# A decoder layer with gated delta-rule attention on one Trainium2 core: block-wise substitution on fewer rows, one sum of squares instead of two, and part of the work moved between engines

## The chip, the cores and the metric

The kernel runs on one core of a Trainium2 chip. A core has TensorE (matmuls; the profile calls it PE, its weight loads PEld), VectorE (DVE), ScalarE (ACT), GpSimd (POOL) and SyncE (SP), which here only issues DMAs. Each engine works through its own queue in order; engines wait for each other by semaphores. The metric is the device time of one execution in microseconds.

## The reference

Input `x` is 16 sequences of 128 tokens with 256 features. The layer is: gated delta-rule attention with 16 key heads and 32 value heads of width 128, then cross attention, then a mixture of experts, each followed by a sum with its input and a layer norm. The change touches the attention alone. Cut to what matters:

```python
mixed = hidden_states @ w_qkv                 # then a causal convolution of 4 taps, silu
q, k, v = jnp.split(mixed, [KEY_DIM, 2 * KEY_DIM], axis=-1)
q = _l2norm(q) * DK ** (-0.5)                 # each key head serves two value heads
k = _l2norm(k)
def step(Sm, inp):
    q_, k_, v_, g_, b_ = inp                  # g_: log of the decay, b_: beta
    Sm = Sm * jnp.exp(g_)[..., None, None]
    kv = jnp.einsum('bhk,bhkv->bhv', k_, Sm)
    delta = (v_ - kv) * b_[..., None]
    Sm = Sm + jnp.einsum('bhk,bhv->bhkv', k_, delta)
    o = jnp.einsum('bhk,bhkv->bhv', q_, Sm)
    return (Sm, o)
og = o * jax.nn.silu(z)
on = og * jax.lax.rsqrt(jnp.mean(og * og, axis=-1, keepdims=True) + EPS) * norm_w
return on.reshape(B, S, VAL_DIM) @ w_out
```

## The kernel before

**Units and steps.** The 128 steps of the recurrence are written as a triangular system of 128 tokens per sequence and head. The work is cut into 64 units: a unit is one key head (with its two value heads, r = 0 and 1) for four sequences (`G` = 4, index b). Four units form a group (`U` = 4). The main loop (from L549) runs over s and works in each step on units of several ages: `a` = unit s (keys, queries, decay, products), `v` (values, six units later), `m`, `p`, `q` (the solution in blocks, seven to nine units later) and `o` (output, ten units later). The order within a step on TensorE, VectorE, ScalarE and SP is chosen by a scheduler when the program is built; GpSimd's order is the order of the code (`manual_schedule`, L548).

**Blocks.** The 128 tokens are four blocks of 32. `products` (L395) makes `lp`, the products of keys with keys and with queries times the decay, and copies the four diagonal 32x32 blocks of the key products to `ldg`. `clear` (L414) then writes zeros over the diagonal blocks 1 to 3 in `lp`, on GpSimd, one step later. What stands above the diagonal is zero by the decay.

**Substitution and solution.** Twice a step, `substitute` (L494) takes off what the blocks before contribute, and `solve` (L510) multiplies with the inverse of the diagonal block. `substitute` has three jobs (unit, r, block st), with st = 1, 2 and 3. For each b and job one matmul (L504) goes to the 32 rows of `pu` that belong to the block. Its operands have all 128 rows: rows of later blocks meet zeros in `lp`. VectorE subtracts `pu` from `u` (L508). `solve` does 16 matmuls (L519) of 32 rows and 32 columns, and ScalarE copies the results back (L523). The profile writes the shape that a matmul takes of the array as rows*columns: L504 is 128*32, L519 is 32*32.

**Inverse.** The inverses of a group's 128 diagonal blocks are made together, one per partition. `begin` (L226) prepares `bp` (beta over the squared norm of the key) and `T` (transposed `ldg`) on VectorE; GpSimd then multiplies `T` by `nbp` (L251), does 30 steps j (`step`, L262: a product and a sum each) and `end` (L271: ones on the diagonal, times `bp`). `turn` (L277) transposes the result on VectorE. The 30 steps are cut into pieces over three steps of the main loop (`piece`, L559). `bp` has one buffer.

**Norms.** `norms` (L370) squares the queries on ScalarE, sums them over the 128 features by four matmuls with ones (`pss`, L377), and VectorE transposes and scales the sums to `ss`. `rms` (L462) sums the squares of the output in the same way (`pms`, L467), with 1/128 as weights, transposes, and adds `ss`; `rms_end` (L476) raises to the power -1/2 on GpSimd, to `rstd`, which VectorE needs for the output (L490). In GpSimd's queue `rms_end` stands behind `piece(0)` and `clear`.

**Output weights.** `scale_wo` (L162) runs in steps 2 to 9: two loads of `w_out`, a multiplication by the norm's weight on GpSimd (L170), two stores to device memory. Its tile shares the one buffer of `og2`.

Of the kernel before, what the change touches and what calls it, by code (L numbers as in the profile page):

```python
# [8 lines left out]
F32 = mybir.dt.float32  # L9
# [32 lines left out]
def decoder_kernel(  # L42
# [16 lines left out]
    ones = const.tile([P, BS], F32, name="ones")  # L59
    pool.memset(ones, 1.0)  # L60
# [56 lines left out]
    with ExitStack() as st:  # L117
# [100 lines left out]
        class Group:  # L218
# [7 lines left out]
            def begin(self):  # L226

                k = self.k

                def small(tag, **kw):  # L230
                    return sb.tile([P, BS], F32, tag=tag, name=f"{tag}{k}", **kw)

                g, h0 = k * U // HK, k * U % HK * 2
                bg = small("bg", bufs=1)
                vec.tensor_copy(bg.rearrange("p (h b) -> p h b", b=G),
                                beta[:, g * G : (g + 1) * G, h0 : h0 + 2 * U]
                                .rearrange("p b h -> p h b"))
                self.bp = bp = small("bp", bufs=1)
                vec.transpose(bp, bg)
# [12 lines left out]
                sst = small("sst", bufs=1)  # L252
                vec.transpose(sst, ss)
                self.sst = sst

# [6 lines left out]
            def step(self, j):  # L262
                T = self.T
                n = BS - 1 - j
                tmp = sb.tile([P, 256], F32, tag="tmp", bufs=1, name=f"tmp{self.k}_{j}")
                tv = tmp[:, : n * j].rearrange("p (i c) -> p i c", c=j)
                pool.tensor_tensor(tv, bc(T[:, j + 1 :, j : j + 1], [P, n, j]),  # L267
                                   bc(T[:, j : j + 1, 0:j], [P, n, j]), ALU.mult)
                pool.tensor_tensor(T[:, j + 1 :, 0:j], T[:, j + 1 :, 0:j], tv, ALU.add)  # L269
# [15 lines left out]
        class Unit:  # L285
# [84 lines left out]
            def norms(self):  # L370

                sq = self.t([P], "sq", bufs=1)
                act.activation(sq, self.kq[:, :, 1, :], AF.Square)
                pss = sm_pool.tile([P, G, BS], F32, tag="sm", name=f"pss{self.n}")
                for i in range(NB):
                    blk = slice(i * BS, (i + 1) * BS)
                    pe.matmul(pss[blk].rearrange("p b t -> p (b t)"), lhsT=ones, rhs=sq[:, :, blk],  # L377
                              start=True, stop=True)
                sst = self.t([BS], "sqt", bufs=1)
                vec.transpose(sst, pss)  # L380
                self.ss = self.t([], "ss", bufs=DELAY + 5)
                vec.tensor_scalar(self.ss, sst[:, :, 0], 1e-6, 1e-6 * P, ALU.add, ALU.mult)
# [30 lines left out]

            def clear(self):  # L414
                for i in range(1, NB):
                    blk = slice(i * BS, (i + 1) * BS)
                    pool.memset(self.lp[blk, :, :, 0, blk].rearrange("p r b t -> p (r b) t"), 0.0)
# [32 lines left out]
            def attend(self, r):  # L450

                if r == 0:
                    self.og = self.t2("og")
                    self.og2 = self.t2("og2", bufs=1)
# [5 lines left out]
                act.activation(self.og2[:, r], self.og[:, r], AF.Square)  # L460

            def rms(self):  # L462

                pms = sm_pool.tile([P, 2, G, BS], F32, tag="sm", name=f"pms{self.n}")
                for i in range(NB):
                    blk = slice(i * BS, (i + 1) * BS)
                    pe.matmul(pms[blk].rearrange("p r b t -> p (r b t)"), lhsT=inv_dv,  # L467
                              rhs=self.og2[:, :, :, blk].rearrange("p r b t -> p (r b) t"),
                              start=True, stop=True)
                mst = sb.tile([P, 2, G, BS], F32, tag="mst", bufs=1, name=f"mst{self.n}")  # L470
                vec.transpose(mst.rearrange("p r b t -> p (r b t)"),
                              pms.rearrange("p r b t -> p (r b t)"))
                self.var = var = sb.tile([P, 2, G], F32, tag="var", name=f"var{self.n}")
                vec.tensor_tensor(var, mst[:, :, :, 0], bc(self.ss[:, None, :], [P, 2, G]), ALU.add)  # L474
# [18 lines left out]

        def substitute(name, jobs):  # L494
# [6 lines left out]
            for b in range(G):  # L501
                for u, r, st in jobs:
                    blk = slice(st * BS, (st + 1) * BS)
                    pe.matmul(pu[blk, b, :], lhsT=u.lp[:, r, b, 0, blk], rhs=u.u_[r][:, b, :],  # L504
                              start=True, stop=True)
# [38 lines left out]
        PIECES = 5  # L544
        done = None


        with tc.manual_schedule(engines={mybir.EngineType.Pool}):  # L548
            for s in range(NU + DELAY + 3):  # L549
# [9 lines left out]
                def piece(i):  # L559
# [3 lines left out]
                    total = 3 * PIECES - 2  # L563
                    if at_ == 0:
                        inv.begin()
                    for j in range(1 + 30 * at_ // total, 1 + min(30, 30 * (at_ + 1) // total)):
                        inv.step(j)
                    if at_ == 2 * PIECES - 1:
                        inv.norms()
                    if at_ == total - 1:  # L570
# [39 lines left out]
                if q is not None:  # L610
                    q.attend(0)
# [14 lines left out]
                if q is not None:  # L626
                    q.attend(1)
                if p is not None:
                    p.gate(1)
                if a is not None:  # L630
                    a.norms()
# [648 lines left out]
```

## Time and profile before

| what | value |
|---|---|
| median of 9 runs | 2244.73 us (2236.57 to 2247.95) |
| profiled execution, own time | 2242.45 us |
| its span, first to last instruction | 2240.4 us |
| granted TensorE clock, mean | 0.969 |
| TensorE's idle time in 300 to 1500 us | 48.4 of 1200 us |
| `pu` (L504) on TensorE, 300 to 1500 us | 2184 passes, 101.4 us |
| `clear` (L417) on GpSimd, 300 to 1500 us | 138 memsets, 42.0 us |
| VectorE's idle time ended by GpSimd's `end` (L275), 300 to 1500 us | 33.0 us, 9 times |
| VectorE's idle time ended by `rstd` (L478), 300 to 1500 us | 43.7 us, 12 times |

The attention takes the first 1797 us; its steady stage begins near 200 us. Cross attention and the experts follow. Times in the traces are microseconds from the span's start. A row of the order in time merges equal instructions that follow each other: start, duration from the first start to the last end, engine, line, operation, written and read tiles, array shape, operand shape, count; in brackets the idle time before and what ended it. Two fp32 passes make one matmul, and each is counted. Matmul ends are modelled and can overlap the next start, so prices below are taken from start to start.

### The profile page before, as it was taken

The page shows a single profiled execution, that of the slowest core. Times are in us where ns is not written, and L with a number is a line of the kernel's source. Part 1 is how long each engine was busy: PE and PEld are TensorE (multiplying, and loading weights), DVE is VectorE, ACT ScalarE, POOL GpSimd, SP SyncE. Part 2 cuts the span into 40 slices and gives each one's busy share as a digit, 9 for nine tenths or more (in the row PEclk, how much of TensorE's full clock was granted, in tenths as well). Part 3 has the DMA queues.
Part 4 walks back from the last instruction along what each step waited for, and adds up shares of the span by engine and source line. Part 5 has one row for each costly group of instructions (what it writes and reads, how often), then busy time and mean ns, then how long its engine had stood idle before and what let it go on. Part 6 is the DMA issues. An engine that isn't in the chain of part 4 may idle for free. (4 is left out here: it accounts for less than half of the span.)

```text
span 2240.4 us, 41392 instructions
## 1 busy us (share of the span) xinstructions
PE 2065.3 (92%) x15128; PEld 1254.5 (56%) x15128; DVE 1747.0 (78%) x3247; ACT 1330.7 (59%) x2692; POOL 1123.8 (50%) x1679
## 2 busy tenths in 40 slices
PE   5659999999999999999999999999999969999997
PEld 3335555555555556555555556555655634448874
DVE  5757888888898888888888888898856667766545
ACT  4646666666666666666666666666655435554431
POOL 1658373646556473829373646556482143252222
PEclk9889999999999999999999999999999979999998
DMA  6332221122222212222221222222111070013321
GB/s 168 109 103 59 66 62 58 58 62 66 57 67 62 57 57 65 64 57 63 61 62 57 57 58 69 60 62 62 34 29 38 20 259 1 1 50 100 105 86 57
DMA packets 140664, 150.78 MB, mean 67 GB/s; under 512 B 14184, under 2 KB 111472, under 8 KB 140464
## 3 DMA queue, kind: packets, MB, share of 16 engines
q1 hardware_dynamic: 135760, 139.56, 21.6%
q0 software_dynamic: 3072, 8.39, 1.2%
q8 instruction: 122, 2.00, 0.4%
q14 instruction: 78, 0.64, 0.1%
q10 hardware_dynamic: 1632, 0.19, 0.1%
HBM read 125.82 MB, written 22.28 MB: 66 GB/s over the span
## 5 line engine op out<-in xcount | busy, mean ns | idle before, releaser
L523 ACT COPY u<-pt 32x512 f32<-32x512 f32 x512 | 294.5, 575 | 63.7 <-PE pt L519 53.7
L359 POOL TENSOR_TENSOR yv<-yv,y2v 128x508 f32<-128x508 f32 x128 | 161.8, 1264 | 272.7 <-DVE yv L351 266.9
L508 DVE TENSOR_TENSOR u<-u,pu 32x512 f32<-32x512 f32 x384 | 263.5, 686 | 33.3 <-PE pu L504 21.5
L490 DVE SCALAR_TENSOR_TENSOR acc<-pp,rstd,acc 128x256 f32<-128x256 f32 x512 | 222.2, 477 | 83.0 <-POOL rstd L478 77.2
L269 POOL TENSOR_TENSOR Tp<-Tp,tmp 128x30 f32<-128x30 f32 (+14 forms) x480 | 266.0, 554 | 37.6
L486 PE MATMUL pp<-wo,og 128*128 128x256 f32 x1024 | 273.8, 394 | 0.0
L334 PE MATMUL pjkq<-xT,wkq 128*128 128x512 f32 x512 | 247.6, 625 | 24.6 <-issue 20.0
L351 DVE SCALAR_TENSOR_TENSOR ykq<-pjkq,cw,ykq 128x500 f32<-128x500 f32 (+2 forms) x384 | 262.7, 726 | 6.1 <-ACT ykq L344 4.3
L334 PE MATMUL pjz<-xT,wz 128*128 128x512 f32 x512 | 251.5, 615 | 12.5 <-DVE yv L351 12.0
L334 PE MATMUL pjv<-xT,wv 128*128 128x512 f32 x512 | 249.7, 610 | 12.1 <-DVE ykq L351 6.6
L267 POOL TENSOR_TENSOR tmp<-Tp 128x30 f32<-128x30 f32 (+14 forms) x480 | 245.9, 512 | 28.2
L351 DVE SCALAR_TENSOR_TENSOR yv<-pjv,cw,yv 128x504 f32<-128x504 f32 (+1 forms) x256 | 188.0, 734 | 66.7 <-ACT y2v L348 62.5
L486 PEld LDWEIGHTS pp<-wo,og 128*128 128x128 f32 x1024 | 182.9, 190 | 84.4 <-issue 62.0
L519 PE MATMUL pt<-u,Tt 32*32 32x128 f32 x4096 | 176.5, 274 | 17.9 <-DVE u L508 17.7
L519 PEld LDWEIGHTS pt<-u,Tt 32*32 32x32 f32 x4096 | 117.1, 105 | 125.1 <-ACT ykq L344 38.7
L360 ACT ACTIVATE vT<-yv 128x512 f32<-128x512 f32 x128 | 80.2, 627 | 168.3 <-POOL yv L359 168.3
L334 PEld LDWEIGHTS pjkq<-xT,wkq 128*128 128x128 f32 x512 | 94.6, 196 | 143.1 <-issue 130.0
L406 DVE TENSOR_TENSOR lp<-pk,e 128x512 f32<-128x512 f32 x256 | 159.4, 681 | 13.9 <-PE pk L403 13.8
L478 POOL TENSOR_TENSOR rstd<-var,m_half 128x8 f32<-128x8 f32 x64 | 105.4, 1648 | 126.0 <-DVE var L474 122.7
L446 ACT ACTIVATE u<-pv,nk 128x128 f32<-128x128 f32 x512 | 149.3, 369 | 32.5 <-PE pv L443 30.6
L389 DVE TENSOR_TENSOR_SCAN e<-dec,ident 128x512 f32<-128x512 f32 x128 | 163.2, 1316 | 2.4 <-DMA dec<-dec_d 0.6
L457 PE MATMUL po<-lp,u 128*128 128x128 f32 x1024 | 147.7, 285 | 17.1 <-DVE acc L490 17.1
(227 smaller groups left out, 3683.0 us busy)
## 6 DMA issues: line engine op xcount, KB each, us to landing
dec<-dec_d SPq DMA_DIRECT2D x64, 512.0 KB, 5.1
wkq<-in_L_attn_w_qkv_dram SPq DMA_DIRECT2D x128, 128.0 KB, 3.5
wv<-in_L_attn_w_qkv_dram SPq DMA_DIRECT2D x64, 256.0 KB, 2.8
wz<-in_L_attn_w_z_dram SPq DMA_DIRECT2D x64, 256.0 KB, 2.7
wo<-wo_d SPq DMA_DIRECT2D x64, 256.0 KB, 2.7
rx<-xg SPq DMA_DIRECT2D x44, 128.0 KB, 2.1
yg<-ry SPq DMA_DIRECT2D x44, 128.0 KB, 1.7
xg<-zero SPq DMA_DIRECT2D x10, 512.0 KB, 8.0
```

What stands on the lines that cost most here:

```text
L267: pool.tensor_tensor(tv, bc(T[:, j + 1 :, j : j + 1], [P, n, j]), bc(T[:, j : j + 1, 0:j], [P, n, j]), ALU.mult)
L269: pool.tensor_tensor(T[:, j + 1 :, 0:j], T[:, j + 1 :, 0:j], tv, ALU.add)
L334: pe.matmul(pj.rearrange("p b t -> p (b t)"), lhsT=ws[kc], rhs=xTs[self.g][:, kc, :], start=(kc == 0), stop=(kc == 1))
L351: vec.scalar_tensor_tensor(out=y[:, :, d:], in0=pj[:, :, : P - d], scalar=c[:, k : k + 1], in1=y[:, :, d:], op0=ALU.mult, op1=ALU.add)
L359: pool.tensor_tensor(y[:, :, 1:], y[:, :, 1:], y2[:, :, 1:], ALU.add)
L389: vec.tensor_tensor_scan(out=e.rearrange("p b t -> p (b t)"), data0=self.dec[:, r, :], data1=ident4.rearrange("p b t -> p (b t)"), initial ...
L406: self.made = vec.tensor_tensor(self.lp[:, r, hf * 2 : hf * 2 + 2], pk, bc(self.e[r][:, hf * 2 : hf * 2 + 2, None, :], [P, 2, 2, P]), ALU. ...
L486: pe.matmul(pp[:, r, :], lhsT=self.og[:, r, b, :], rhs=self.wo[:, r, :], start=True, stop=True)
L490: vec.scalar_tensor_tensor(out=a, in0=pp[:, r, :], scalar=self.rstd[:, r, b : b + 1], in1=a, op0=ALU.mult, op1=ALU.add)
L508: vec.tensor_tensor(u.u_[r][blk], u.u_[r][blk], pu[blk], ALU.subtract)
L519: pe.matmul(pt[blk, b, :], lhsT=groups[u.n // U].Tt[blk, 8 * u.u + G * r + b, :], rhs=u.u_[r][blk, b, :], start=True, stop=True)
L523: act.copy(u.u_[r][blk], pt[blk])
```

## The change

- `bp` has two buffers.
- `clear` is gone. `substitute` reads only the rows ahead of the block: 32, 64 or 96 of 128.
- `norms` and `rms` become `square` and `sums`: the squares of the output of one unit and of the queries of another lie in one tile (`sqs`), and one set of four matmuls over up to 384 columns and one transpose serve both. It runs in the step after, between `decay` and `key_query(0)`. The matmuls take 1/128 as weights for both, and `ss` is scaled to match; the tile `ones` is gone.
- `rms_end` stands ahead of `piece(0)` in GpSimd's queue.
- The negation (`T` times `nbp`) is a method of its own. For group 0 it and steps 1 to 15 run on VectorE, in piece 0, and steps 16 to 30 on GpSimd in pieces 1 to 8. For the other groups the negation stands in piece 1, and the 30 steps in pieces 1 to 12.
- `scale_wo` multiplies on ScalarE, with the two buffers of `og`.

```diff
-    ones = const.tile([P, BS], F32, name="ones")
-    pool.memset(ones, 1.0)
...
-            wor = sb.tile([P, 2, G, P], F32, tag="og2", bufs=1, name=f"wor{i}")
+            wor = sb.tile([P, 2, G, P], F32, tag="og", name=f"wor{i}")
...
-            pool.tensor_scalar(wor, wor, normw, None, ALU.mult)
+            act.activation(wor, wor, AF.Copy, scale=normw)
...
-                self.bp = bp = small("bp", bufs=1)
+                self.bp = bp = small("bp")
...
-                pool.tensor_tensor(self.T, self.T, bc(nbp[:, None, :], [P, BS, BS]), ALU.mult)
+                self.nbp = nbp
...
+            def negate(self, eng):
+                eng.tensor_tensor(self.T, self.T, bc(self.nbp[:, None, :], [P, BS, BS]), ALU.mult)
...
-            def step(self, j):
+            def step(self, j, eng):
...
-            def norms(self):
-                sq = self.t([P], "sq", bufs=1)
-                act.activation(sq, self.kq[:, :, 1, :], AF.Square)
...
+            def square(self, sqs):
+                act.activation(sqs, self.kq[:, :, 1, :], AF.Square)
...
-            def clear(self):
-                for i in range(1, NB):
-                    blk = slice(i * BS, (i + 1) * BS)
-                    pool.memset(self.lp[blk, :, :, 0, blk].rearrange("p r b t -> p (r b) t"), 0.0)
...
+        def sums(name, sqs, o, a):
+            lo, hi = (0 if o is not None else 2), (3 if a is not None else 2)
+            psq = sm_pool.tile([P, 3, G, BS], F32, tag="sm", name=f"psq{name}")
+            for i in range(NB):
+                blk = slice(i * BS, (i + 1) * BS)
+                pe.matmul(psq[blk, lo:hi].rearrange("p r b t -> p (r b t)"), lhsT=inv_dv,
+                          rhs=sqs[:, lo:hi, :, blk].rearrange("p r b t -> p (r b) t"),
+                          start=True, stop=True)
+            mst = sb.tile([P, 3, G, BS], F32, tag="mst", bufs=1, name=f"mst{name}")
+            vec.transpose(mst[:, lo:hi].rearrange("p r b t -> p (r b t)"),
+                          psq[:, lo:hi].rearrange("p r b t -> p (r b t)"))
+            if o is not None:
+                o.var = sb.tile([P, 2, G], F32, tag="var", name=f"var{name}")
+                vec.tensor_tensor(o.var, mst[:, 0:2, :, 0], bc(o.ss[:, None, :], [P, 2, G]), ALU.add)
+            if a is not None:
+                a.ss = sb.tile([P, G], F32, tag="ss", bufs=DELAY + 5, name=f"ss{name}")
+                vec.tensor_scalar(a.ss, mst[:, 2, :, 0], 1e-6 / P, 1e-6 * P * P, ALU.add, ALU.mult)
...
-                    pe.matmul(pu[blk, b, :], lhsT=u.lp[:, r, b, 0, blk], rhs=u.u_[r][:, b, :],
-                              start=True, stop=True)
+                    pe.matmul(pu[blk, b, :], lhsT=u.lp[: st * BS, r, b, 0, blk],
+                              rhs=u.u_[r][: st * BS, b, :], start=True, stop=True)
...
+                    n0, last = (15, 8) if k == 0 else (0, 3 * PIECES - 3)
                     if at_ == 0:
                         inv.begin()
+                        if k == 0:
+                            inv.negate(vec)
+                            for j in range(1, 1 + n0):
+                                inv.step(j, vec)
+                        return
+                    if at_ == 1 and k > 0:
+                        inv.negate(pool)
+                    if at_ > last:
+                        return
+                    for j in range(1 + n0 + (30 - n0) * (at_ - 1) // last,
+                                   1 + n0 + (30 - n0) * at_ // last):
+                        inv.step(j, pool)
...
-                if o is not None:
-                    o.rms()
+                if o is not None or at(s - 1) is not None:
+                    sums(s, sqs, o, at(s - 1))
...
-                piece(0)
-                if s > 0 and at(s - 1) is not None:
-                    at(s - 1).clear()
                 if o is not None:
                     o.rms_end()
+                piece(0)
```

More of the change, by code (lines that the diff above doesn't have):

```diff
@@ L266, in step @@
                 tv = tmp[:, : n * j].rearrange("p (i c) -> p i c", c=j)
-                pool.tensor_tensor(tv, bc(T[:, j + 1 :, j : j + 1], [P, n, j]),
+                eng.tensor_tensor(tv, bc(T[:, j + 1 :, j : j + 1], [P, n, j]),
                                    bc(T[:, j : j + 1, 0:j], [P, n, j]), ALU.mult)
-                pool.tensor_tensor(T[:, j + 1 :, 0:j], T[:, j + 1 :, 0:j], tv, ALU.add)
+                eng.tensor_tensor(T[:, j + 1 :, 0:j], T[:, j + 1 :, 0:j], tv, ALU.add)
             def end(self):
@@ L368, in key_query @@
                 self.conv(f"kq{i}", ws, chunk, out)
-            def norms(self):
-                sq = self.t([P], "sq", bufs=1)
-                act.activation(sq, self.kq[:, :, 1, :], AF.Square)
-                pss = sm_pool.tile([P, G, BS], F32, tag="sm", name=f"pss{self.n}")
-                for i in range(NB):
-                    blk = slice(i * BS, (i + 1) * BS)
-                    pe.matmul(pss[blk].rearrange("p b t -> p (b t)"), lhsT=ones, rhs=sq[:, :, blk],
-                              start=True, stop=True)
[L379 to L382, printed above, removed]
+            def square(self, sqs):
+                act.activation(sqs, self.kq[:, :, 1, :], AF.Square)
             def decay(self):
@@ L412, in products @@
                     act.copy(grp.ldg[blk, 8 * self.u : 8 * self.u + 8, :], d)
-            def clear(self):
-                for i in range(1, NB):
-                    blk = slice(i * BS, (i + 1) * BS)
-                    pool.memset(self.lp[blk, :, :, 0, blk].rearrange("p r b t -> p (r b) t"), 0.0)
             def value(self, r):
@@ L447, in values, with attend @@
                 self.u_[r] = v
-            def attend(self, r):
+            def attend(self, r, sqs):
                 if r == 0:
                     self.og = self.t2("og")
-                    self.og2 = self.t2("og2", bufs=1)
                 po = self.bank(f"po{r}")
@@ L459, in attend @@
                 vec.tensor_tensor(self.og[:, r], po, self.zs[r], ALU.mult)
[L460 to L474, printed above, removed]
+                act.activation(sqs, self.og[:, r], AF.Square)
             def rms_end(self):
@@ L503, in substitute @@
                     blk = slice(st * BS, (st + 1) * BS)
-                    pe.matmul(pu[blk, b, :], lhsT=u.lp[:, r, b, 0, blk], rhs=u.u_[r][:, b, :],
-                              start=True, stop=True)
+                    pe.matmul(pu[blk, b, :], lhsT=u.lp[: st * BS, r, b, 0, blk],
+                              rhs=u.u_[r][: st * BS, b, :], start=True, stop=True)
             for u, r, st in jobs:
@@ L544, in decoder_kernel @@
         PIECES = 5
+        sqs = None
         done = None
@@ L562, in piece @@
                     at_ = ph * PIECES + i
-                    total = 3 * PIECES - 2
+                    n0, last = (15, 8) if k == 0 else (0, 3 * PIECES - 3)
                     if at_ == 0:
                         inv.begin()
-                    for j in range(1 + 30 * at_ // total, 1 + min(30, 30 * (at_ + 1) // total)):
-                        inv.step(j)
-                    if at_ == 2 * PIECES - 1:
+                        if k == 0:
[10 more added lines that the diff above has]
+                        inv.step(j, pool)
+                    if at_ == min(last, 2 * PIECES - 1):
                         inv.norms()
-                    if at_ == total - 1:
+                    if at_ == last:
                         inv.end()
@@ L594, in decoder_kernel @@
                     a.decay()
-                if o is not None:
-                    o.rms()
+                if o is not None or at(s - 1) is not None:
+                    sums(s, sqs, o, at(s - 1))
+                if a is not None or q is not None:
+                    sqs = sb.tile([P, 3, G, P], F32, tag="og2", bufs=1, name=f"sqs{s}")
                 if a is not None:
                     a.key_query(0)
-                piece(0)
-                if s > 0 and at(s - 1) is not None:
-                    at(s - 1).clear()
                 if o is not None:
                     o.rms_end()
+                piece(0)
                 if a is not None:
@@ L610, in decoder_kernel @@
                 if q is not None:
-                    q.attend(0)
+                    q.attend(0, sqs[:, 0])
                 if v is not None:
@@ L626, in decoder_kernel @@
                 if q is not None:
-                    q.attend(1)
+                    q.attend(1, sqs[:, 1])
                 if p is not None:
@@ L630, in decoder_kernel @@
                 if a is not None:
-                    a.norms()
+                    a.square(sqs[:, 2])
                     a.products(ga)
```

## The prediction, made before the changed kernel ran

> **What bounds the kernel now.** I read the page first (engines, then the 40 slices), then busy time by stage, then what TensorE waited for in the steady stage, and last the order in time on TensorE's matmul and weight rows.
>
> ```profile
> PE 2065.3 (92%) x15128; PEld 1254.5 (56%) x15128; DVE 1747.0 (78%) x3247; ACT 1330.7 (59%) x2692; POOL 1123.8 (50%) x1679
> ...
> PE   5659999999999999999999999999999969999997
> ```
>
> TensorE is full from the fourth slice on; only the first three slices (some 170 us) have room. By stage (columns: PE, PEld, DVE, ACT, POOL, granted clock, DMA share, GB/s):
>
> ```profile
> 134.00:200.00 66.00, 56.98 (x376) 30.47 (x376) 50.46 (x73) 41.59 (x89) 40.42 (x56) 0.95 0.32 92
> 240.00:1740.00 1500.00, 1436.03 (x11475) 872.43 (x11469) 1271.71 (x2181) 984.68 (x1984) 839.89 (x1233) 0.99 0.21 58
> 300.00:1500.00 1200.00, 1151.60 (x9172) 699.44 (x9171) 1042.31 (x1782) 795.83 (x1603) 683.21 (x1011) 0.99 0.22 61
> ```
>
> In 240 to 1740 us TensorE is busy 1436 of 1500 us, VectorE 1272, GpSimd 840. A step (one unit of 64) lasts 26 us and TensorE idles 1.1 us of it. So what relieves VectorE, ScalarE or GpSimd can gain no more than those 64 us there, and every microsecond put on TensorE is paid in full. What TensorE waited for in 300 to 1500 (engine, line, releaser: us in total, times, longest):
>
> ```profile
> PE po L457 <- DVE acc L490: 14.4, 11, 1.4
> PE pt L519 <- DVE u L508: 12.8, 24, 1.1
> PE pv L443 <- ACT vT L360: 10.2, 7, 1.5
> PE pjz L334 <- DVE yv L351: 10.1, 11, 0.9
> ```
>
> Now the price of small matmuls. Each is two passes (x24 for twelve matmuls).
>
> ```profile
> 713.75 1.07 PE L504 MATMUL pu<-u,lp 128*32 128x128 f32 x24
> 714.75 0.70 PE L486 MATMUL pp<-wo,og 128*128 128x256 f32 x2
> ...
> 188.67 0.41 PE L504 MATMUL pu<-u,lp 128*32 128x128 f32 x2
> 189.01 0.40 PE L519 MATMUL pt<-u,Tt 32*32 32x128 f32 x2
> 189.34 1.32 PE L504 MATMUL pu<-u,lp 128*32 128x128 f32 x22
> ```
>
> Start to start, twelve `pu` matmuls of one shape take 714.75 - 713.75 = 1.00 us, 0.083 each: three column strips of the array run at once. But one `pu` (shape 128*32) followed by one `pt` (32*32) takes 0.34 us, and back again 0.33, though the two use different strips. The weight row shows why:
>
> ```profile
> 188.67 0.14 PEld L504 LDWEIGHTS pu<-u,lp 128*32 128x32 f32 x2
> 189.00 0.13 PEld L519 LDWEIGHTS pt<-u,Tt 32*32 32x32 f32 x2 [0.20 <-issue]
> 189.34 1.06 PEld L504 LDWEIGHTS pu<-u,lp 128*32 128x32 f32 x22 [0.20 <-issue]
> ```
>
> At a change of shape the next weights aren't loaded until the running matmul is through (0.20 us of empty weight row, ended by no other engine). At 161.80, 162.10, 162.44 the same pattern has 0.30 and 0.34.
>
> **No clearing of blocks** (`clear`, `substitute`). `substitute` reads 32, 64 or 96 rows instead of 128. As built, its three jobs then have the shapes 32*32, 64*32 and 128*32, and the loop is over the four batches outside and the jobs inside: the shape changes at every one of the twelve matmuls of a call. Taken at the measured 0.335 us for an isolated one, a call costs 12 x 0.335 = 4.02 us instead of 1.00. There are 1536 such matmuls (64 units x 24): 1536 x (0.335 - 0.083) = **+387 us**. The trace shows 128*32 to 32*32 and back; it shows neither 32*32 to 64*32 nor 64*32 to 128*32. Upper bound 0.34 each: +394. Lower bound: nothing, as between strips of one shape (0.083). I take the upper side: all other changes of shape that I looked at (128*128 to 128*32, 128*32 to 32*32, 32*32 to 128*128) have the same 0.17 to 0.20 us gap in the weight row, and these two are of that kind. The page "TensorEngine Tiling (Array Packing)" of the Trainium skill, section "Key Properties", speaks against this edit: changing the tiling mode, and not just the tile, drains the TensorE; it lists 32x32, 64x32 and 128x32 as different modes. By its rule all twelve drain (+387 us as above); by the same-shape row alone the edit would cost TensorE nothing. The drains cover nothing and nothing covers them in the steady stage; only in the first five calls (134 to 200 us, 48 matmuls, TensorE idle 9 of 66 us) I hide half: 48 x 0.252 / 2 = **-6**. GpSimd saves three memsets of 0.30 us a unit, off TensorE's path: 0.
>
> **What frees TensorE's waits.** Two buffers for `bp`: VectorE no longer waits for GpSimd's last multiplication of the group before (33.0 us in nine waits in 300 to 1500). The power of the output norm ahead of the inverse's piece and of its wait for the negation: VectorE's `acc` no longer waits for `rstd` (43.7 us there). On TensorE these can show only in the rows above, `po` and `pjz` (24.5 of 48.3 us in 46 steps). Besides, every step gets 6 us longer for the other engines while their work stays, so part of the waits for `u` and `vT` goes too. I take 60% of the 64 us: **-38** (bounds 0 and -64). ScalarE's and VectorE's queues have that room: DVE 1272 in what would be some 1850 us.
>
> **Squares summed together.** `pss` (8 passes, 0.35 us: 725.73 to 726.08) and `pms` (8 passes: six took 0.56) become one call with 384 columns. Four strips run at once, so a call is two passes of a strip and 0.13 us around them: `pss` 2 x 0.107 + 0.13 = 0.34 and `pms` 2 x 0.213 + 0.13 = 0.56 fit; 384 columns give 2 x 0.32 + 0.13 = 0.77, that is 0.14 less than the two. x 64 = **-9** (bounds 0 and 64 x 0.35 = -22). VectorE's two transposes (450 and 314 ns) become one, about 590: hidden. The sum moves ahead of `key_query` of the next step; its consumer `ss` is used ten steps later.
>
> **Start: first inverse half on VectorE, weights scaled on ScalarE, `bp`.** (a) VectorE stood still for `bp` here:
>
> ```profile
> 132.29 0.21 DVE L239 STREAM_TRANSPOSE bp<-bg 128x32 f32<-128x32 f32 x1 [21.70 <-POOL Tp L275]
> ```
>
> But group 0 is needed anyway before unit 0 can be solved. What VectorE did between GpSimd's end (132.25) and the transpose `Tt` (138.41) can now come before: -6 at most. (b) Steps 1 to 15 and the negation leave GpSimd, where the whole took 77.96 to 132.25. On VectorE they are 30 instructions of 30 to 240 elements, at 0.18 (128x32) to 0.40 us (between 0.29 at 128 and 0.68 at 512 elements) 9.6 us, and 1.25 for the negation. They stand in VectorE's queue between the products and scans of units 4 to 6, the last behind the scan of unit 6, which puts the handing over at about 111. GpSimd's rest is 104.74 to 130.10 less a scaling (2.85) and a clearing (1.02), and 2.1 for the end: 23.6 us, so 134.6 against 132.25: +2. (c) `scale_wo` on ScalarE: its first scaling stands ahead of the first sigmoid in ScalarE's queue, behind which are all of unit 0's evictions. The loads are issued at 9.1 and 10.0 and land 7.0 us later, at 17.0; with about 1.05 us for 128x1024 (0.63 for 128x512) and 1.28 for the table, `beta` comes at 19.4 instead of 15.0: +4.4. The next scalings also wait for loads that stand in SP's queue behind stores and weights, and the stores stand ahead of the loads of `dec`, for which VectorE's scan waits. I take +7 (bounds 0, as VectorE is busy only 36 of the first 60 us, and +14). Together **+3** (bounds -8 and +16).
>
> **Sum.** 2240.4 (span) + 387 - 6 - 38 - 9 + 3 = 2577; the execution's own time is 2.05 us above its span (2242.45), and the median of nine runs 2.3 above that (2244.73). Forecast: **2580 us**. Its own range is 2500 to 2640 (0.30 to 0.35 us a matmul gives +333 to +410; the waits 0 to -64; start -8 to +16).
>
> **Rivals.**
> 1. *No drain between shapes of equal width* (on the other side). The three jobs use disjoint column strips; if the array takes weights for another number of rows while a strip streams, `pu` stays at 1.00 us and the gains stand alone: 2240.4 - 38 - 9 + 3 + 4.3 = 2201 us. For it: strips overlap in every `pu` call. Against it: at 188.67 to 189.34 the strips were disjoint too, and it drained. It decides below 0.083 + 44/1536 = 0.11 us a matmul.
> 2. *Two of three changes drain* (64*32 and 128*32 count as one kind, or 32*32 and 64*32 do). Four rounds of 2 x 0.335 make a call 2.68 us: 128 calls x 1.68 = +215, so 2416.
> 3. *One drain in a round* (only the known change from 128*32 to 32*32): 4 x 0.335 = 1.34 a call, 128 x 0.34 = +44, so about 2245: no change, the gains eaten.
> 4. *The start decides.* If nothing drains and ScalarE's waits for loads add their full 14 us, that is 2212: it only shifts rival 1.
>
> **How the numbers follow.** Forecast 0.77, rival 1 (with 4) 0.13, rival 2 0.06, rival 3 0.04. The range takes in rival 2 and leaves out most of rivals 1 and 3: 2395 to 2640. Some 0.2% (5 us) is what the nine runs, 2236.57 to 2247.95, can tell from no change. Faster: rival 1 and a third of 3: 0.14; same: 0.02; slower: 0.84.
>
> **What would show it.** Right: `pu` start to start 4 us a call, its matmuls in ones, a gap of 0.2 us in the weight row before each; a step of 31 to 32 us; DVE, ACT and POOL shares lower at equal busy time; no wait of `bp` for `Tp`, `acc` hardly waiting for `rstd`; first `beta` near 19 us. Wrong: `pu` as one block of 1.0 us and a step of 25 us (rival 1), or blocks of 1.3 or 2.7 us (rivals 3 and 2). The prediction stands or falls with two changes of shape that this trace does not show.

## The result and the profile after

| | before | after |
|---|---|---|
| median | 2244.49 us (31 runs, 2236.57 to 2251.48) | 2626.23 us (10 runs, 2606.89 to 2644.10) |
| ratio, 95% interval | 1 | 1.1703 [1.1677, 1.1728] |
| profiled execution, own time | 2242.45 us | 2610.43 us |
| its span, mean granted clock | 2240.4 us, 0.969 | 2608.3 us, 0.940 |

The changed kernel is 17% slower; the forecast was 2580, in a range of 2395 to 2640. The page of the changed kernel, engines and slices:

```profile
PE 2498.4 (96%) x14688; PEld 1386.6 (53%) x14688; DVE 1727.8 (66%) x3223; ACT 1335.5 (51%) x2700; POOL 991.4 (38%) x1447
...
PE   5689999999999999999999999999999997999998
...
PEclk8879999998999989999989999999999988999998
```

TensorE has 440 fewer passes and 433 us more busy time. VectorE and ScalarE have nearly the busy time they had, in a longer span, so their shares fell. The third row, the granted clock in tenths, differs too. Before it read:

```profile
PEclk9889999999999999999999999999999979999998
```

In the stage where before every slice had a 9, the changed kernel has an 8 every few slices. The same by stage (PE, PEld, DVE, ACT, POOL, granted clock, DMA share, GB/s):

```profile
134.00:200.00 66.00, 56.61 (x285) 26.88 (x286) 40.68 (x63) 34.61 (x75) 29.72 (x40) 0.78 0.13 37
240.00:1740.00 1500.00, 1497.51 (x9028) 815.99 (x9028) 1052.13 (x1781) 813.98 (x1645) 620.27 (x875) 0.96 0.18 50
300.00:1500.00 1200.00, 1198.23 (x7206) 653.64 (x7204) 836.24 (x1419) 648.66 (x1309) 513.05 (x732) 0.95 0.18 50
```

TensorE idles 1.8 of 1200 us, where it was 48.4. All that it waited for in that stage is one row:

```profile
PE pjv L335 <- issue: 1.8, 5, 0.4
```

The four waits shown of before are gone. A step is longer all the same, and the order in time on TensorE says by what:

```profile
713.16 4.07 PE L494 MATMUL pu<-u,lp 32*32 32x128 f32 x24
717.15 1.13 PE L456 MATMUL pp<-wo,og 128*128 128x256 f32 x4
...
726.77 4.07 PE L494 MATMUL pu<-u,lp 32*32 32x128 f32 x24
730.77 0.66 PE L428 MATMUL pv<-ident,vT 128*128 128x128 f32 x4
731.36 0.85 PE L471 MATMUL psq<-sqs,inv_dv 128*32 128x384 f32 x8
732.14 1.13 PE L335 MATMUL pjkq<-xT,wkq 128*128 128x512 f32 x2
```

The twelve `pu` matmuls take 717.15 - 713.16 = 3.99 us (4.00 the second time), where they took 1.00; `psq` takes 732.14 - 731.36 = 0.78. The rows merge what has one line and name the first shape only; the weight row keeps the shapes apart:

```profile
713.49 0.13 PEld L494 LDWEIGHTS pu<-u,lp 64*32 64x32 f32 x2 [0.20 <-ACT sqs L444]
713.82 0.14 PEld L494 LDWEIGHTS pu<-u,lp 96*32 96x32 f32 x2 [0.20 <-issue]
714.15 0.13 PEld L494 LDWEIGHTS pu<-u,lp 32*32 32x32 f32 x2 [0.20 <-issue]
714.49 0.13 PEld L494 LDWEIGHTS pu<-u,lp 64*32 64x32 f32 x2 [0.20 <-issue]
```

Each matmul starts 0.33 us after the one before it, with 0.20 us of empty weight row between, at all three changes of shape (the prediction's 128*32 appears as 96*32). The trace has a control inside itself, at 167.8 us, where `pu` and `pt` happen to meet with one shape:

```profile
167.79 0.29 PE L494 MATMUL pu<-u,lp 32*32 32x128 f32 x1 [1.89 <-ACT u L513]
167.80 0.29 PE L509 MATMUL pt<-u,Tt 32*32 32x128 f32 x1
167.92 0.27 PE L494 MATMUL pu<-u,lp 32*32 32x128 f32 x1
167.93 0.27 PE L509 MATMUL pt<-u,Tt 32*32 32x128 f32 x1
```

They start 0.01 us apart and run together. Before, the like pair had two shapes, 128*32 and 32*32, and was 0.30 us apart:

```profile
161.80 0.38 PE L504 MATMUL pu<-u,lp 128*32 128x128 f32 x2 [2.01 <-ACT u L523]
162.10 0.40 PE L519 MATMUL pt<-u,Tt 32*32 32x128 f32 x2
```

So it is the change of shape that costs, not the place.

The attention ends (first row of its last layer norm) at 2169.70 instead of 1800.33 us: +369. What follows takes 438.6 instead of 440.1. The start of the changed kernel, on ScalarE:

```profile
15.84 1.15 ACT L168 ACTIVATE wor<-wor,normw 128x1024 f32<-128x1024 f32 x1 [6.40 <-DMA wor<-in_L_attn_w_out_dram]
18.30 0.28 ACT L192 ACTIVATE beta<-pab 128x128 f32<-128x128 f32 x1
```

ScalarE waits 6.40 us for the load of the first output weights, and `beta` comes at 18.30 instead of 15.00.

**The clock.** Three steps of the changed kernel, as stretches of the same view (same columns as by stage):

```profile
701.49:731.36 29.87, 29.87 (x194) 16.53 (x193) 22.42 (x44) 17.24 (x35) 21.66 (x28) 1.00 0.21 54
731.36:762.87 31.51, 31.51 (x194) 17.44 (x193) 24.69 (x42) 17.46 (x35) 13.48 (x22) 0.95 0.19 51
571.48:605.43 33.95, 33.95 (x193) 18.32 (x192) 21.38 (x37) 17.45 (x35) 21.69 (x28) 0.87 0.17 48
```

TensorE's 193 or 194 passes take 29.87 us at a granted clock of 1.00, 31.51 at 0.95, 33.95 at 0.87. Inside the second of them, around its first `pu` call, in three stretches of 3.41 us and then in the order of time:

```profile
743.40:746.81 3.41, 3.41 (x22) 1.43 (x22) 0.12 (x1) 0.86 (x2) 2.78 (x10) 1.00 0.00 0
746.81:750.22 3.41, 3.41 (x8) 2.17 (x8) 2.81 (x5) 0.06 (x1) 2.62 (x2) 0.50 0.00 0
750.22:753.63 3.41, 3.41 (x41) 2.09 (x41) 1.68 (x4) 2.02 (x4) 0.00 (x0) 1.00 0.26 79
```

```profile
743.03 4.21 PE L494 MATMUL pu<-u,lp 32*32 32x128 f32 x24
747.17 2.07 PE L456 MATMUL pp<-wo,og 128*128 128x256 f32 x4
749.04 2.47 PE L335 MATMUL pjv<-xT,wv 128*128 128x512 f32 x4
```

The drained call covers the whole of the first stretch. Near its end the clock goes to one half and stays there for 3.41 us. What stands behind the call pays: the four `pp` passes take 1.87 us, where at 717.15 they took 0.97. Not every call is followed by this: of the 20 steps from 380.70 to 1022.64 us, 15 were below 1.00, most of them at 0.94 to 0.98, which is one dip for two calls.

The trace holds every change of the granted clock, and these show when a call is followed by a dip. In 300 to 1500 us 26 dips begin, each to 0.50, 20 of them for 3.41 us and six for twice that, and all begin on one grid of 3.413 us. Before each of them lies a window of that grid of which a single `pu` call covers 88% or more. The other 49 calls cover no window beyond 89%. So for these calls it depends on where the 4.0 us of a call fall on the grid. The kernel before has five dips of 3.41 us in the same stage, each behind 3.41 us in which TensorE was busy for 1.22 to 2.00 us and otherwise stood still.

The page "TensorE: Matmul & The Clock Gate" of the Trainium skill, Part 1, has windows of 3413 ns that run on freely, and half the clock after one in which the array was idle. The length of the dips and the grid agree with that. But here the array isn't idle in the call; by the profile it is busy all the time.

### The profile page after: what moved, and what is told of

Same layout as the page of the kernel before. It is cut to its first block, busy times and chain, and to the rows that moved or that the text cites. A ratio compares the mean times of both kernels' runs of the same rounds, so it can differ in the third digit from the quotient of the medians.

```text
span 2608.3 us, 40050 instructions
## 1 busy us (share of the span) xinstructions
PE 2498.4 (96%) x14688; PEld 1386.6 (53%) x14688; DVE 1727.8 (66%) x3223; ACT 1335.5 (51%) x2700; POOL 991.4 (38%) x1447
## 4 chain that ended last, share of the span: by engine, by line
PE 91%; DVE 3%; POOL 2%; ACT 1%; DMA 1%; issue 1%; SPq 0%; ACTq 0%; POOLq 0%; DVEq 0%
PE pu L494 20%; PE pp L456 10%; PE pjv L335 9%; PE pjkq L335 9%; PE pjz L335 9%; PE pt L509 6%; PE po L441 5%; PE pk L393 4%; PE pv L428 3%; PE psc L770 2%; PE psq L471 2%; PE prg L1106 1%; PE prd L1106 1%; PE pru L1106 1%; PE pav L807 1%
## 5 line engine op out<-in xcount | busy, mean ns | idle before, releaser
L494 PE MATMUL pu<-u,lp 32*32 32x128 f32 (+2 forms) x3072 | 532.1, 287 | 3.1 <-ACT u L513 3.1
L494 PEld LDWEIGHTS pu<-u,lp 32*32 32x32 f32 (+2 forms) x3072 | 209.3, 106 | 336.2 <-issue 290.4
L456 PE MATMUL pp<-wo,og 128*128 128x256 f32 x1024 | 300.9, 427 | 0.0
L335 PE MATMUL pjkq<-xT,wkq 128*128 128x512 f32 x512 | 258.5, 647 | 26.2 <-issue 21.9
L268 POOL TENSOR_TENSOR tmp<-Tp 128x240 f32<-128x240 f32 (+14 forms) x465 | 225.6, 485 | 142.2 <-DVE Tp L270 112.8
L352 DVE SCALAR_TENSOR_TENSOR ykq<-pjkq,cw,ykq 128x504 f32<-128x504 f32 (+2 forms) x384 | 268.1, 728 | 16.6 <-ACT ykq L345 15.5
L460 DVE SCALAR_TENSOR_TENSOR acc<-pp,rstd,acc 128x256 f32<-128x256 f32 x512 | 234.0, 478 | 63.7 <-PE pp L456 48.3
L335 PE MATMUL pjv<-xT,wv 128*128 128x512 f32 x512 | 263.3, 641 | 13.0 <-issue 12.9
L270 POOL TENSOR_TENSOR Tp<-Tp,tmp 128x240 f32<-128x240 f32 (+14 forms) x465 | 241.0, 518 | 36.5
L456 PEld LDWEIGHTS pp<-wo,og 128*128 128x128 f32 x1024 | 199.3, 207 | 88.5 <-issue 66.4
```

The source lines that it names most:

```text
L268: eng.tensor_tensor(tv, bc(T[:, j + 1 :, j : j + 1], [P, n, j]), bc(T[:, j : j + 1, 0:j], [P, n, j]), ALU.mult)
L270: eng.tensor_tensor(T[:, j + 1 :, 0:j], T[:, j + 1 :, 0:j], tv, ALU.add)
L335: pe.matmul(pj.rearrange("p b t -> p (b t)"), lhsT=ws[kc], rhs=xTs[self.g][:, kc, :], start=(kc == 0), stop=(kc == 1))
L352: vec.scalar_tensor_tensor(out=y[:, :, d:], in0=pj[:, :, : P - d], scalar=c[:, k : k + 1], in1=y[:, :, d:], op0=ALU.mult, op1=ALU.add)
L456: pe.matmul(pp[:, r, :], lhsT=self.og[:, r, b, :], rhs=self.wo[:, r, :], start=True, stop=True)
L460: vec.scalar_tensor_tensor(out=a, in0=pp[:, r, :], scalar=self.rstd[:, r, b : b + 1], in1=a, op0=ALU.mult, op1=ALU.add)
```

## The experiments

Twelve kernels on chips whose times of the kernel before differ (2265.78 us for the first four, 2246.01 for the next four, 2269.06 for the last), so only ratios to the kernel before on the same chip are compared. Steps can be set side by side, since the chips differ behind the attention: `r2_power_behind` and `x1_scale_pool`, on two chips, start their last power at 1748.32 and 1747.97 us and end their span at 2193.1 and 2214.9. The step is the mean of 52 in the profiled execution: from the second to the fifteenth time that GpSimd sets the diagonal of `T`, once in four steps. The clock is that granted in 300 to 1500 us.

| kernel | ratio [95%] | step, us | clock |
|---|---|---|---|
| before | 1 | 26.24 | 0.99 |
| after | 1.1703 [1.1677, 1.1728] | 31.95 | 0.95 |
| e1_full_rows | 1.0000 [0.9989, 1.0011] | 26.22 | 1.00 |
| e2_uncleared | 0.9861 [0.9841, 0.9881] | 25.68 | 1.00 |
| e3_before_short | 1.1547 [1.1522, 1.1572] | 31.68 | 0.97 |
| e4_job_outside | 1.0678 [1.0654, 1.0702] | 28.61 | 1.00 |
| w1_clear_late | 0.9874 [0.9858, 0.9891] | 25.71 | 1.00 |
| r2_power_behind | 0.9770 [0.9755, 0.9784] | 25.30 | 1.00 |
| r3_scale_pool | 0.9999 [0.9987, 1.0012] | 26.25 | 1.00 |
| r4_inverse_pool | 0.9989 [0.9981, 0.9998] | 26.22 | 1.00 |
| b1_bp_one | 0.9767 [0.9753, 0.9780] | 25.31 | 1.00 |
| x1_scale_pool | 0.9770 [0.9757, 0.9784] | 25.31 | 1.00 |
| x2_clear_late | 0.9703 [0.9690, 0.9717] | 25.04 | 1.00 |
| c1_twice | 1.2616 [1.2597, 1.2636] | 35.54 | 1.00 |

### Is it the fewer rows?

`e1_full_rows` is the changed kernel with 128 rows and the clearing.

```diff
+                if s > 0 and at(s - 1) is not None:
+                    at(s - 1).clear()
...
-                    pe.matmul(pu[blk, b, :], lhsT=u.lp[: st * BS, r, b, 0, blk],
-                              rhs=u.u_[r][: st * BS, b, :], start=True, stop=True)
+                    pe.matmul(pu[blk, b, :], lhsT=u.lp[:, r, b, 0, blk],
+                              rhs=u.u_[r][:, b, :], start=True, stop=True)
```

> The changed kernel with all its parts, but with the clearing back (behind piece 0 and the power in GpSimd's queue) and 128 rows again in substitute: one array shape for all of its matmuls. Theory (the changes of shape drain TensorE): pu about 1.0 us a call in one block, a step of some 25.0 us, 2185 to 2215 us, and the granted clock back at 0.965 or above. Rival (the merged sum or the moved work slows the step, the shapes do little): above 2450 us.

1.0000. The whole loss is gone and `pu` takes 1.00 us again (705.90 to 706.90), but the gain of the other parts that I had added up isn't there. `e2_uncleared` is the same without the clearing (it leaves out the zeros on the diagonal blocks):

> The changed kernel with 128 rows in substitute and without the clearing; it leaves out the zeros on the diagonal blocks. Theory: clearing lies beside other work on GpSimd, so the time is that of the run with the clearing within 0.3%. Rival (clearing delays the power or the values through GpSimd's queue): 0.5% or more faster than with it.

0.9861: the rival. Three memsets a unit that I had costed at nothing are worth 1.4% where they stand. `e3_before_short` is the kernel before with the fewer rows and without the clearing, and nothing else:

```diff
-                    pe.matmul(pu[blk, b, :], lhsT=u.lp[:, r, b, 0, blk], rhs=u.u_[r][:, b, :],
-                              start=True, stop=True)
+                    pe.matmul(pu[blk, b, :], lhsT=u.lp[: st * BS, r, b, 0, blk],
+                              rhs=u.u_[r][: st * BS, b, :], start=True, stop=True)
...
-                if s > 0 and at(s - 1) is not None:
-                    at(s - 1).clear()
```

> The kernel before with one edit: substitute reads 32, 64 and 96 rows and the clearing is gone. Theory: +387 us of drains, less up to 64 us of TensorE's waits, plus a lower granted clock (0.92 to 0.945) that adds some 40 us: 2590 to 2660 us, within 2% of the changed kernel. Rival (the loss needs the other parts of the change): below 2450 us.

1.1547, with the lowered clock too (0.97). This one edit makes nearly all of the loss. Its stage shows one thing more:

```profile
300.00:1500.00 1200.00, 1199.99 (x7602) 654.01 (x7595) 861.01 (x1482) 662.97 (x1332) 529.63 (x743) 0.97 0.19 51
```

TensorE idles 0.01 of 1200 us, although this kernel has one buffer for `bp` and the power in its old place. `e4_job_outside` leaves the rows as changed and swaps the loops, so that the shape changes three times in a call and not twelve:

```diff
-            for b in range(G):
-                for u, r, st in jobs:
+            for u, r, st in jobs:
+                for b in range(G):
```

> The changed kernel with the two loops of substitute exchanged: jobs outside, batches inside. Shapes change three times a call instead of twelve, but the four matmuls of a job go to one column strip and can't overlap. Theory (a group of one shape takes its passes in series at 0.107 us and 0.13 us around them): 3 x (8 x 0.107 + 0.13) = 2.96 us a call instead of 4.0, 128 x 1.04 = 133 us less than the changed kernel, 2470 to 2510 us. Rival (only the number of changes of shape counts, strips don't): 3 x 0.335 or little more a call, about 2250 us. Rival (reading fewer rows is itself slow): no difference, 2600 us or more.

Its order in time on TensorE:

```profile
705.51 3.04 PE L494 MATMUL pu<-u,lp 32*32 32x128 f32 x24
708.47 1.13 PE L456 MATMUL pp<-wo,og 128*128 128x256 f32 x4
```

The call takes 2.96 us, as worked out. The ratio, 1.0678 (2397 us at the first chip's 2244.49), is far below what I expected, since I had started from a step of the changed kernel with its lowered clock, and here the clock is 1.00.

### Does the emptied array lower the clock?

`c1_twice` issues every `pu` matmul twice in a row; the shape still changes twelve times a call.

```diff
-                    pe.matmul(pu[blk, b, :], lhsT=u.lp[: st * BS, r, b, 0, blk],
-                              rhs=u.u_[r][: st * BS, b, :], start=True, stop=True)
+                    for _ in range(2):
+                        pe.matmul(pu[blk, b, :], lhsT=u.lp[: st * BS, r, b, 0, blk],
+                                  rhs=u.u_[r][: st * BS, b, :], start=True, stop=True)
```

> The changed kernel with every matmul of the substitution issued twice in a row, the second with the same operands into the same place: the changes of shape stay, and the calls hold twice the work. The call: 12 x (0.335 + 0.083) = 5.0 us instead of 4.0, 128 us more in 128 calls, ratio 1.227 at an unchanged clock. Theory (the clock falls in the changed kernel because TensorE does little in a call that drains twelve times): the granted clock in 300 to 1500 us rises from 0.95 to 0.98 or more and the ratio is 1.215 or less. Rival (the draining itself, or the length of the call, lowers the clock): 0.95 or less, ratio 1.225 or more.

The stage of 300 to 1500 us, and a call:

```profile
300.00:1500.00 1200.00, 1196.76 (x8115) 734.78 (x8112) 753.22 (x1292) 590.13 (x1185) 464.53 (x658) 1.00 0.17 45
```

```profile
718.43 6.69 PE L495 MATMUL pu<-u,lp 32*32 32x128 f32 x48
725.05 0.66 PE L428 MATMUL pv<-ident,vT 128*128 128x128 f32 x4
```

The clock is 1.00, as the theory has it. The time is a miss: the call takes 6.62 us and not 5.0, and so the ratio, 1.2616, lies where the rival put it, though not by a lowered clock. A repeat on the strip of the matmul before costs 0.22 us, where 0.083 holds between different strips. So neither the draining nor the length of the call lowers the clock by itself; with the same twelve gaps of 0.20 us, weights are loaded in 64% of the time (0.35 of 0.55 us a pair) instead of 39% (0.13 of 0.33). That the little work in a window is what counts fits this, the dips of the kernel before, and `e4_job_outside`, whose calls of 2.96 us cover 87% of a window at most. But `e1_full_rows` waits as much as the kernel before and has no dip, so TensorE's idle time alone doesn't decide; what measure of work the chip takes isn't shown. Nor was the changed kernel run on the chip of `c1_twice`. The dips are not those of one chip, though: `e3_before_short`, on another than the changed kernel's, has 17 in the stage, each behind a window that a call covers to 86% or more (two of its other 66 calls cover 94% and 97% and have none).

### Where did the gain of the other parts go?

In `e1_full_rows` TensorE idled 57.8 of 1200 us in 300 to 1500, against 48.4 before. Its largest waits there, and one value on ScalarE:

```profile
PE pv L433 <- ACT vT L361: 14.7, 24, 0.8
PE pv L433 <- DVE acc L465: 14.0, 21, 0.8
```

```profile
726.93 0.63 ACT L361 ACTIVATE vT<-yv 128x512 f32<-128x512 f32 x1 [6.54 <-POOL yv L360]
```

`po` no longer waits for `acc`. In its place stands `pv`, which waits as long for `vT` and for `acc`; `vT` in its turn waited 6.54 us for GpSimd's sum `yv`. GpSimd's queue around the power, in the same kernel (rows of the inverse between are left out):

```profile
708.50 0.60 POOL L270 TENSOR_TENSOR Tp<-Tp,tmp 128x210 f32<-128x210 f32 x1
713.11 1.65 POOL L453 TENSOR_TENSOR rstd<-var,m_half 128x8 f32<-128x8 f32 x1 [4.00 <-DVE ss L487]
...
717.51 1.02 POOL L408 MEMSET lp<- 32x256 f32 x3
...
725.64 1.26 POOL L360 TENSOR_TENSOR yv<-yv,y2v 128x508 f32<-128x508 f32 x1
```

GpSimd stands still for 4.00 us because the power is next in its queue and its input isn't there; two steps of the inverse, the clearing, more of the inverse and then `yv` are queued behind it. Four kernels each change one thing in `e1_full_rows`.

`w1_clear_late` moves the clearing behind the last piece:

```diff
-                if s > 0 and at(s - 1) is not None:
-                    at(s - 1).clear()
...
                 piece(4)
+                if a is not None:
+                    a.clear()
```

> The kernel with all its rows and with the clearing, but the clearing moved from behind the first piece of the next step to behind the last piece of its own step, where GpSimd then stands idle for 3 to 11 us before the power. Theory (what GpSimd has to do ahead of the value sum decides two steps of every four, and the clearing is 1.07 us of it there): the ratio to the kernel before is that of the kernel without clearing, 0.986 to 0.989, and four steps take 102.8 us instead of 104.9. Rival (the zeros themselves cost, by the writes into lp or by the waits they hang on others): four steps stay at 104.9 us and the ratio at 1.000.

0.9874: as without clearing (0.9861). The zeros cost next to nothing, their place in the queue does. `r2_power_behind` puts the power where it was before the change:

```diff
-                if o is not None:
-                    o.rms_end()
                 piece(0)
                 if s > 0 and at(s - 1) is not None:
                     at(s - 1).clear()
+                if o is not None:
+                    o.rms_end()
```

> All rows and the clearing where it was before; the power back behind the first piece and the clearing. In the full-row kernel GpSimd stands still 2.9 to 11.3 us a step for the variance, with the first piece (2 or 3 steps of the inverse, 2.6 to 4 us) and the clearing (1.02 us) queued behind it. Theory (power first is a loss, because that idle time is no longer filled and the value sum comes later): four steps take 102.8 us or less instead of 104.9, ratio 0.984 to 0.990. Rival (power first is a gain, since the accumulation on VectorE waits for rstd): four steps take 105.5 us or more, as in the kernel before, ratio 1.002 to 1.006.

0.9770, more than the theory gave it. The same place in its GpSimd queue:

```profile
724.47 0.48 POOL L270 TENSOR_TENSOR Tp<-Tp,tmp 128x150 f32<-128x150 f32 x1
725.01 1.02 POOL L408 MEMSET lp<- 32x256 f32 x3
726.11 1.65 POOL L453 TENSOR_TENSOR rstd<-var,m_half 128x8 f32<-128x8 f32 x1
```

No idle time before the power. VectorE waits for it again:

```profile
DVE acc L465 <- POOL rstd L453: 18.4, 12, 1.9
```

That is 18.4 us in 1200, against 43.7 before and none in `e1_full_rows`, and it is much the cheaper wait. The power first is a loss of 2.3%.

`r3_scale_pool` scales the output weights on GpSimd again:

```diff
-            act.activation(wor, wor, AF.Copy, scale=normw)
+            pool.tensor_scalar(wor, wor, normw, None, ALU.mult)
```

> All rows and the clearing; the output weights are scaled on GpSimd again, not on ScalarE. Theory (the scaling ahead of beta on ScalarE's queue is most of the late start, beta 18.5 us instead of 15.0, and so the first inverse): the first inverse is cleared at about 130 to 133 us instead of 137.7, everything after it comes 3 to 5 us earlier, ratio 0.998. Rival (the half inverse on VectorE decides the start): the first clearing stays at 136 us or later and the ratio at 1.000.

`beta` comes at 13.94 us and the first diagonal is set at 128.79 instead of 137.67 us, a little more than expected; but the second comes only 4.1 us earlier and the last power 1.95 us earlier. In the time nothing is to be seen. `r4_inverse_pool` makes the whole first inverse on GpSimd:

```diff
-                    n0, last = (15, 8) if k == 0 else (0, 3 * PIECES - 3)
+                    n0, last = 0, 3 * PIECES - 3
...
-                        if k == 0:
-                            inv.negate(vec)
-                            for j in range(1, 1 + n0):
-                                inv.step(j, vec)
...
-                    if at_ == 1 and k > 0:
+                    if at_ == 1:
```

> All rows and the clearing; the whole first inverse on GpSimd, in twelve pieces. Theory (the half on VectorE buys nothing, since it starts only behind the loads and holds up VectorE's queue): the first inverse ends within 2 us of 137.7, ratio 0.999 to 1.000. Rival 1 (the half on VectorE is worth having): the first inverse ends 6 us or more later, at 144 us or after, ratio 1.003 or more. Rival 2 (VectorE is what the start waits for): the second group's inverse, cleared at 225.6 us, comes 5 us or more earlier, ratio 0.997.

The first inverse is ready 2.8 us earlier than with the half on VectorE (134.88; more than the 2 us that the theory allowed), the second at the same time (225.45 and 225.60). 0.9989 is just told from no change. The half on VectorE is worth nothing or a little less.

### What remains, and a version that beats both

`b1_bp_one` is `r2_power_behind` with one buffer for beta.

```diff
-                self.bp = bp = small("bp")
+                self.bp = bp = small("bp", bufs=1)
```

> All rows, the clearing and the power as before (the kernel of 0.977, four steps in 101.0 us), but one buffer for a group's beta. Theory (the second buffer takes off VectorE's queue a wait that GpSimd's last use of beta ended, 33.0 us of VectorE in 1200 before, up to 3.9 us once in four steps): four steps take 102.0 to 104.9 us, ratio 0.985 to 1.000. Rival (the gain is that of the squares summed together; VectorE's wait lies beside TensorE's work): four steps stay at 101.0 us within 0.3, ratio 0.976 to 0.979.

0.9767, step 25.31: the rival. The second buffer is worth nothing here. `x1_scale_pool` is `r2_power_behind` with the edit of `r3_scale_pool`, and `x2_clear_late` adds to that the edit of `w1_clear_late`:

> As the kernel of 0.977, with the output weights scaled on GpSimd again. With the power first this brought the end of the attention 2 us earlier (last power at 1794.1 instead of 1796.0 us). Theory (the late start is partly taken up again by the fourth group): 2 to 4 us faster, ratio 0.975 to 0.976. Rival (with GpSimd's queue in its old order the scaling there delays the first steps as it did before): ratio 0.977 or more.

> As the last one, and the clearing moved behind the last piece of its own step. Theory (with the power behind the first piece TensorE is 98% busy, the rest of its idle time is put down to issue and not to a wait, so GpSimd's queue no longer decides): the same time within 0.2%. Rival (VectorE still waits 18.4 us in 1200 for the power, which comes 1.07 us earlier without the clearing ahead of it): 0.4 to 0.8% faster than the last one.

0.9770 is no gain, so the rival. 0.9703, on the other hand, is 0.6% better (2203.33 after 2217.43 us), the rival as well: `acc`'s wait for the power fell to 7.8 us. The stage in `x2_clear_late`:

```profile
300.00:1500.00 1200.00, 1186.74 (x9235) 725.25 (x9234) 1086.12 (x1827) 823.71 (x1683) 702.19 (x1057) 1.00 0.23 64
```

TensorE is busy 98.9%. This kernel keeps of the change the second buffer, the squares summed together and the pieces of the inverse with the first half on VectorE; it has all rows, the clearing at the end of its own step, the power in its old place and the scaling on GpSimd. At 2203.33 against 2269.06 us on its chip it is faster than both kernels.

## Why the prediction was right, and where it was not

**The drains: right, in size too.** 0.335 us for each of twelve matmuls, 4.02 a call, was taken from a change between 128*32 and 32*32; 0.33 and 3.99 to 4.00 were measured, also for the two changes that the old trace didn't show. 128 x 2.99 = 383 us instead of 387. `e1_full_rows`, `e3_before_short` and `e4_job_outside` show it from three sides. Of the two rules that the prediction weighed, the Trainium skill's ("TensorEngine Tiling (Array Packing)", Key Properties: changing the tiling mode drains TensorE) was the right one here, and not the same-shape row. The third shape is 96*32 in the profile, not 128*32 as the prediction had it; it drains like the others. The -6 for the first five calls can't be told apart; their stage, 134 to 200 us, has a granted clock of 0.78 instead of 0.95.

**The clock: not in the sum at all.** That is the step that failed. The prediction's own rows show 0.99 for the stage, and it never asks what the drained calls do to that. Without the lowered clock a step would be 35.54 - 2 x (6.62 - 3.99) = 30.28 us by `c1_twice`, or 28.61 + 2 x (3.99 - 2.96) = 30.67 by `e4_job_outside`, instead of 31.95. So it costs 1.3 to 1.7 us a step, some 82 to 107 us in 64. The granted clock of the two spans says much the same without any of the other kernels: 2608.3 x 0.060 = 156.5 us against 2240.4 x 0.031 = 69.5, which is 87 us more. It also makes the scatter of the ten runs: their spans go from 2604.8 us (clock 0.939) to 2642.0 (0.924), but span times clock stays between 2441 and 2449 us.

**The waits: more than 60% went.** Term -38, bounds 0 and -64. A step went from 26.24 to 31.95, +5.71; the drains are 2 x 2.99 = 5.98 of it, the sums -0.14, the clock 1.3 to 1.7, which leaves -1.4 to -1.8 a step, 90 to 115 us. The idle time that the profile shows (48.4 of 1200 us, 1.06 a step) went almost entirely (1.8, 0.05 a step). The term starts from the second buffer of `bp` and the power ahead, and names last that each step is longer for the other engines. `e3_before_short`, which has only the last, idles 0.01 of 1200 us: the longer step does it alone. That leaves 0.4 to 0.8 us a step beyond the idle time, out of time that the profile counts as busy. 0.2 of it is what the kernel before lost to its own clock (five dips, 8.5 us in 1200); what the rest is stays open. The forecast thus owes some of its closeness to luck, two errors of opposite sign: +82 to +107 for the clock, -52 to -77 for the waits.

**The squares summed together.** 0.77 us was expected, 0.78 measured; the term of -9 is that. But from the kernel before to `b1_bp_one` a step falls by 0.93 us, far more than 0.14. In the traces 0.51 of the 0.93 is TensorE's idle time (48.4 and 26.0 of 1200 us) and 0.2 the lowered clock of the kernel before. `b1_bp_one` differs by the sums, their place, the pieces of the inverse, the first group, and the scaling of the output weights, which is worth nothing by `x1_scale_pool`. So the gain lies in one or several of the others; they weren't tried one by one.

**The start.** +3 (from -6, +2 and +7). `beta` came at 18.3 (19.4 expected), the half inverse cost 2.8 where +2 was said (`r4_inverse_pool`), the scaling 8.9 at the first inverse where +7 was said (`r3_scale_pool`), the second buffer nothing where up to -6 was said (`b1_bp_one`). The first `pt` stands at 145.94 instead of 141.64 us, +4.3. Most of it is taken up again: `e1_full_rows` ends its last power 0.5 us after the kernel before.

**"GpSimd saves three memsets, off TensorE's path: 0" and the power first.** Both were wrong as statements on the kernel without drains, and hidden in the changed one, whose TensorE waits for nothing. With all rows the clearing costs 1.3% where it stands (`w1_clear_late`) and the power first costs 2.3% (`r2_power_behind`): the prediction asked who waits for the power, and not who is queued behind it while it waits. Rival 1's 2201 us, for no drains and no clearing, is answered by `e2_uncleared`: 0.9861 x 2244.49 = 2213 us.

**The other rivals.** Full calls of 1.3 or 2.7 us (3 and 2) don't occur in the steady stage, and rival 4 supposes that nothing drains.

**What would show it.** Calls of 4 us with 0.2 us gaps, a step of 31 to 32 (31.95), lower shares of the other engines, no wait for `bp` and `acc` waiting only for `pp`: all seen. Only GpSimd's busy time didn't stay equal; it fell from 1123.8 to 991.4 us.

## What to carry to other kernels

Fewer rows in a matmul saved nothing here (32, 64 and 96 rows all took 0.33 us), and where matmuls of different shapes alternate, each change is paid in full: keep one shape in a run, with padding zeros if need be, rather than exact operands. An instruction moved to the front of a queue in program order is judged by what stands behind it while its own input is missing; work that nobody awaits (the clearing) belongs where the engine stands still anyway. And when a change adds short, emptied stretches to TensorE, count the granted clock of what comes after them.

## What was not expected of the hardware

- After a `pu` call that drains twelve times in 4 us, the granted clock can go to 0.50 for 3.41 us, although TensorE counts as busy throughout. It does so where the call covers nearly all of a window (88% or more) on a grid of 3.413 us, and so in some steps and not in others. The times of the changed kernel scatter by 37 us in 10 runs, those of the kernel before by 15 in 31.
- With the repeated matmuls of `c1_twice`, in a call 2.6 us longer with as many drains, the clock stays at 1.00.
- A matmul of two passes follows one on its own strip after 0.22 us (`c1_twice`), one on another strip in the same shape after 0.083 (the `pu` calls of the kernel before).
